# Set-up of quaternions, rows and rotation at other places, second batch's quotients on ScalarE, coefficients copied by GpSimd

## The chip, the cores and the metric

The kernel runs on 1 core of one Trainium2 chip. The metric is the device time of one execution in microseconds. The five engines of a core are named as in the profile: PE is TensorE (matmuls; PEld its weight loads), DVE is VectorE, ACT is ScalarE, POOL is GpSimd, and SP is SyncE, which here issues DMAs. Each engine works through its own instructions in order and waits on the others by semaphores.

## What is computed

Four layers are added to x (8 batches of 256 rows by 256 channels, fp32), one after another. The reference, cut to what matters:

```
def _tc_rmsnorm(x, t, gw, gb, bw, bb):
    g = (t @ gw.T + gb)[:, None, :]; b = (t @ bw.T + bb)[:, None, :]
    return g * x * rsqrt(mean(x * x, -1) + EPS) + b

# layer 0
x = x + _attention(_tc_rmsnorm(x, t, g1w, ...), Wq, Wk, Wv, Wo)        # 16 heads of 16
x0 = x + _swiglu(_tc_rmsnorm(x, t, g2w, ...), gate_w, hid_w, out_w)    # hidden 1024
# layer 1: masked attention, its output normed, scaled and shifted by cond
mod = silu(conditioning) @ Wc.T + bc
x1 = xn * (1.0 + sc[:, None, :]) + shift[:, None, :]
# layer 2: rotation by quaternions, every channel of 4 x 64
q_right_n = _normalize(q_right); q_left_n = _normalize(q_left)
x_rotated = hamilton(q_left_n, hamilton(x_filtered, conj(q_right_n)))
# layer 3: top 2 of 8 experts by a router, each a 3-layer MLP of width 512
return einsum('bseh,bse->bsh', out_e, cw)
```

Layer 2 is one 4 by 4 matrix for each of the 64 quaternion channels; `cond_256` serves as q_left. The kernel builds that matrix once, while the first batches run.

## The kernel before

A batch of 256 rows is worked on as two tiles of 128 partitions. Layer 0's and layer 1's attentions of all batches are cut into blocks (one half of the heads and one half of the keys): a block issues 8 score products s_a into PSUM (L988) and one exponential on ScalarE (L990); the values o_a follow a block later (L1001), and four VectorE instructions turn, divide and turn back the result (tu, inv, on, oT, L1010 to L1018). A function `run` issues a list of blocks. After each block it takes pieces of other work (projections, swiglu products) from a generator until a budget of microseconds is used up; `beside` holds generators of which one step is issued after a given block; `soon` is how many pieces are issued ahead of the function that closes an attention (`after_first`, L1094, or `after_second`, L1164: the outward projection py and what depends on it).

Up to the end of the second step (six blocks: the last two of the second batch, four of the third), the order in which PE, VectorE, ScalarE and GpSimd get their instructions is the order of the program's text; after that only that of PE, VectorE and ScalarE. So a step that is moved in the text is moved in each engine's queue.

The pieces the diff touches:

- `first_norm(b)`, L1045: a batch's first norm in three parts: the squares of two tiles (L878), an rsqrt of 11 small VectorE instructions (L619 to L624: rq_v, rq_y, then three rounds of three), and the quotients xs (L900 on ScalarE, L902 on VectorE or GpSimd).
- `first(b)`: transposes xs, scales it to xT (L924), then projects k (copy kT on ScalarE, L942), q (two products by a scalar on VectorE, qz, L946) and v (copy va on ScalarE, L957). Scores need qz and kT.
- `prepare_quaternions`: squares and sums both quaternions, an rsqrt, four products (19 VectorE instructions), then 32 copies of one column each on GpSimd into lm and rm (L784, L786).
- `set_up_rotation`, a generator of four parts: the matrix rot and the router's share of it on VectorE (L791 to L820), the DMAs that write its coefficients to memory and read them back for all partitions (L822, L824); then the copy to coef (L829) and the products pmc for layer 1's modulation, moved to SBUF as mc (L834); then hall (L851); then shg.
- `set_up_rows`: five iotas on GpSimd and two casts on VectorE for the tables of expert tiles, which are made from round 6 on.
- `second_step`, a generator whose steps are issued beside the six blocks of the second step; between the rotation's parts it takes the fourth batch's norm (`first_turned(3)`), whose row of rstd goes to memory and back by two DMAs (L1063, L1065) and is multiplied in at L1071 (xr).

The banks of PSUM that projections, pmc, pg, ph and phall go to are three, used in turn; a product waits until the bank three before it has been read.

```
        g0 = first(0)
        next(g0)
        keep_busy(2)
        scales()
        do(first_norm(1))
        for _ in g0:
            pass
```

Of the kernel before, what the change touches and what calls it, by code (L numbers as in the profile page):

```python
# [493 lines left out]
def block_kernel(ctx: ExitStack, tc: tile.TileContext, a: dict, out: bass.AP):  # L494
    nc = tc.nc
# [308 lines left out]
    def set_up_rotation():  # L804
        prepare_rotation()

        nc.vector.tensor_tensor(
            wg4s, part["wg4"].rearrange("p (j e) -> p j e", e=E),
            part["rms4"].unsqueeze(2).to_broadcast([P, 4, E]), ALU.mult,
        )  # L810
        for h in range(2):
            r = slice(h * C, (h + 1) * C)
            nc.vector.tensor_copy(rmine[r], rotg[r].rearrange("p j (k h) -> p k h j", h=2)[:, :, h, :])
        turned = work.tile([P, KC, 4, E], F32, tag="raw", bufs=2, name="turned")
        nc.vector.tensor_tensor(
            turned, rmine.unsqueeze(3).to_broadcast([P, KC, 4, E]),
            wg4s.unsqueeze(1).to_broadcast([P, KC, 4, E]), ALU.mult,
        )
        nc.vector.tensor_reduce(gall, turned.rearrange("p k j e -> p k e j"), AX.X, ALU.add)
        nc.vector.tensor_copy(wv1[:, :, D:], gall)  # L820

        nc.sync.dma_start(out=coef_row, in_=rotg[0:C].rearrange("c j i -> c (j i)"))  # L822
        rows_in = wt("x4", [P, C, 4, 4], "coef_in", 1)
        nc.sync.dma_start(  # L824
            out=rows_in.rearrange("p c j i -> p (c j i)"),
            in_=coef_row.rearrange("c w -> (c w)").partition_broadcast(P),
        )
        yield
        nc.scalar.copy(coef, rows_in.rearrange("p c j i -> p i j c"))  # L829

        pm = bank("pmc", (P, 2 * KC, B))
        for k in range(2 * KC):
            nc.tensor.matmul(pm[:, k, :], wcT[:, k * P : (k + 1) * P], silu_c, start=True, stop=True)
        nc.vector.tensor_tensor(mc, pm, part["bcc"].unsqueeze(2).to_broadcast([P, 2 * KC, B]), ALU.add)  # L834
        nc.vector.scalar_tensor_tensor(
            mc[:, KC:], mc[:, KC:], 1.0, part["rsc"].unsqueeze(2).to_broadcast([P, KC, B]), ALU.add, ALU.mult
        )
        scaled = wt("mod", [P, KC, B, E], "scaled")
        nc.vector.tensor_tensor(
            scaled, mc[:, KC:].unsqueeze(3).to_broadcast([P, KC, B, E]),  # L840
            gall.unsqueeze(2).to_broadcast([P, KC, B, E]), ALU.mult,
        )
        yield
        ph = bank("phall", (P, KC, B * E))
        for c in range(KC):
            for k in range(KC):
                nc.tensor.matmul(
                    ph[:, c, :], wo1n[:, k, c * P : (c + 1) * P], scaled[:, k].rearrange("p b e -> p (b e)"),
                    start=k == 0, stop=k == KC - 1,
                )  # L850
        nc.vector.tensor_copy(hall.rearrange("p k b e -> p k (b e)"), ph)  # L851
        ps = bank("pshift", (B, E))
        for k in range(KC):
            nc.tensor.matmul(ps, mc[:, k, :], gall[:, k, :], start=k == 0, stop=k == KC - 1)
        each = work.tile([B, B, E], F32, tag="r_each", bufs=1, name="each")
        nc.vector.tensor_tensor(
            each, ps.unsqueeze(1).to_broadcast([B, B, E]),
            ident[0:B, 0:B].unsqueeze(2).to_broadcast([B, B, E]), ALU.mult,
        )
        yield  # L860
        pb = bank("pshg", (P, B * E))
        nc.tensor.matmul(pb, ones[0:B, :], each.rearrange("p b e -> p (b e)"), start=True, stop=True)
        nc.vector.tensor_copy(shg.rearrange("p b e -> p (b e)"), pb)
        yield
# [172 lines left out]
    def do(parts):  # L1037
        for _ in parts:
            pass
# [5 lines left out]
    def first_norm(b):  # L1045
        s = state[b]
        s["x"] = xs_in.pop(b)
        yield from normed(
            lambda xs: s.update(xs1=xs), s["x"], f"n1_{b}", (nc.scalar, nc.scalar) if b == 0 else (nc.vector, nc.scalar) if b == 1 else nc.gpsimd,
            (nc.scalar, nc.scalar if b else nc.vector),  # L1050
        )

# [287 lines left out]
    def set_up_rows():  # L1340
        full = row("fulli", [NJ, len(BOUNDS)], I32)
        for i, bound in enumerate(BOUNDS):
            nc.gpsimd.iota(full[:, :, i], [[SL, NJ]], base=bound, channel_multiplier=0)
        rows["full"] = row("full", [NJ, len(BOUNDS)])
        nc.vector.tensor_copy(rows["full"], full)
        rows["tno"] = iota_row("tno", NBIG, 1)
# [403 lines left out]
    def chain(*gens):  # L1750
        for g in gens:
            yield from g
# [33 lines left out]
    def once(f, *args):  # L1786
        f(*args)
        yield

    def at_once(*gens):  # L1790
        for g in gens:
            for _ in g:
                pass
        yield
# [10 lines left out]
    with tc.manual_schedule(engines=by_text):  # L1805
        unread = ps_o.tile([P, P], F32, tag="o", name="unread")
        keep_busy(9)
        n1 = first_norm(0)
        next(n1)
        next(n1)  # L1810
        set_up_factors(0)
        set_up_factors(2)
        do(n1)
        keep_busy(3)
        g0 = first(0)
        next(g0)
        keep_busy(2)
        scales()
        do(first_norm(1))
        for _ in g0:  # L1820
            pass
        blank = set_up_slots()
        prepare_condition()
        cond_g = prepare_router()
        finish_slots(*blank)
        def third(b):

            operand = first(b)
            yield next(operand)
            yield from set_up_router(cond_g)  # L1830
            yield from operand

        def take(n, pieces):
            for _ in range(n):
                yield next(pieces)


        operands = first(1)
        run("b", chain(take(1, operands), set_up_condition(), set_up_router(cond_g)), 9.0, rest=False)
        run("b", take(1, operands), 9.0, {0: [at_once(first_norm(2))]}, rest=False)  # L1840
        run("b", iter(()), 0.0)
        run("b", operands, 9.0, rest=False)
        operands = first(2)
        then = run("b", iter(()), 0.0, hold=True)
        run("b", take(1, operands), 9.0, owed=then, soon=1, rest=False)

        def second_step():
            set_up_rows()
            prepare_quaternions()
            yield  # L1850
            rotation = set_up_rotation()
            next(rotation)
            yield
            n1 = first_turned(3)
            next(n1)
            next(n1)
            next(rotation)
            yield
            do(n1)
            next(rotation)  # L1860
            set_up_ones()
            yield
            yield from rotation

        set_up = second_step()
        gaps = [1.9, 4.0, 7.2, 7.2, 7.2, 7.2]
        run("bbbbbb", chain(operands, others(0)), gaps, {n: [set_up] for n in range(5)})
    by_text = {mybir.EngineType.DVE, mybir.EngineType.Activation}
    text_order = ctx.enter_context(ExitStack())
    text_order.enter_context(tc.manual_schedule(engines=by_text))  # L1870
# [1 line left out]
    for i in range(2, B - 1):  # L1872

        placed = {
            2: lambda: once(compare_queries), 4: lambda: at_once(place_choices(0)),
            6: lambda: at_once(place_choices(1)),
        }.get(i, lambda: iter(()))()
        last, rotated = rotated, rotate(i - 2)
        n1 = first_turned(i + 2) if i + 2 < B else iter(())
        n2, r1 = in_parts(i, "n2"), in_parts(i - 2, "r1")  # L1880
        gaps = [7.6, 5.7, 3.8, 5.7, 8.2, 3.8, 2.5, 3.8] if i + 2 < B else [7.6, 3.8, 1.9, 5.7, 7.6, 1.2, 1.9, 3.8]
        starts = {0: [last, n1], 1: [last, n2], 2: [n2]}
        beside = {
            0: [last, n1], 1: [last, n2], 2: [n1], 3: [last], 4: [placed], 5: [r1], 6: [rotated],
            7: [rotated, rotated],
        }
        if i == B - 2:

            early = table("early", (NG - 2) * NTG, EARLY, ALU.is_ge)
            for t in (4, 7):  # L1890
                beside[t].append(early)
        run("bbbbbbbb", others(i - 1), gaps, beside, late_=() if i + 2 < B else (4,), starts=starts)


    pieces = others(B - 2)
# [7 lines left out]
        pl, "s", EARLY, near_end=(next(others_[0]) for _ in range(1)),  # L1903
    )
    n2 = in_parts(B - 1, "n2")
    run("bbbvn", pieces, 3.8, {0: [n2], 2: [early], 3: [early]}, soon=3, rest=False, starts={0: [n2], 1: [n2]})

    next(pieces)
    next(pieces)
# [192 lines left out]
```

## Time and profile before

| what | us |
|---|---|
| median of 5 runs | 711.0 |
| lowest and highest | 707.83, 713.07 |
| the profiled execution, device time | 711.29 |
| its span in the profile | 709.5 |
| VectorE, ScalarE, GpSimd busy | 367.2, 257.2, 178.4 |

The granted TensorE clock over the span is 0.994 of full speed. Times in rows of the profile are microseconds from the span's start; a row gives start, length, engine, line, operation, output and inputs with shapes, and how often it stands there in a row. The part that the diff touches first lies between 9 and 77 us (first two steps), the last one at 384 to 398 us (end of the seventh batch's swiglu).

### The profile page before, as it was taken

What the parts mean: (1) busy time and instruction counts of PE and PEld (TensorE: products, weight loads), DVE (VectorE), ACT (ScalarE), POOL (GpSimd) and SP (SyncE); (2) the same over time, 40 slices, a digit from 0 to 9 for tenths busy, and PEclk for the clock granted to TensorE, in tenths of its full rate; (3) what the DMA queues carried; (4) which work ended last, traced back from release to release, by engine and by line L of the source; (5) the groups of instructions that cost most, each with busy time, mean ns of one, the idle gap of its engine ahead of it and who ended that gap; (6) DMA issues with size and microseconds to landing.
All of it is one profiled execution on the core that took longest, in us unless ns stands there. A gap on an engine that the chain in (4) does not pass through costs nothing.

```text
span 709.5 us, 11183 instructions
## 1 busy us (share of the span) xinstructions
PE 690.1 (97%) x4258; PEld 531.0 (75%) x4258; DVE 367.2 (52%) x1166; ACT 257.2 (36%) x411; POOL 178.4 (25%) x222
## 2 busy tenths in 40 slices
PE   9979999999999999999999999999999999999994
PEld 7546876766766766766676786688888998999894
DVE  5474346476478486377575686688321222222221
ACT  4655135345354354355434335322111212222220
POOL 5330501001000141100230016224373332342213
PEclk9999999999999999999999999999999999999998
DMA  9414001002021000020000151737585866576712
GB/s 298 151 33 80 1 1 38 1 16 38 1 75 38 1 18 7 1 75 1 2 16 1 25 193 25 290 130 213 144 274 158 239 232 204 168 259 199 249 25 29
DMA packets 28879, 70.02 MB, mean 99 GB/s; under 512 B 9032, under 2 KB 22224, under 8 KB 26384
## 3 DMA queue, kind: packets, MB, share of 16 engines
q1 hardware_dynamic: 20032, 57.70, 25.0%
q0 software_dynamic: 8496, 11.32, 7.2%
q8 instruction: 35, 0.57, 0.3%
q14 instruction: 28, 0.23, 0.1%
q10 hardware_dynamic: 288, 0.18, 0.1%
HBM read 59.67 MB, written 9.53 MB: 98 GB/s over the span
## 4 chain that ended last, share of the span: by engine, by line
PE 83%; DVE 7%; DMA 2%; issue 1%; ACT 1%; POOL 1%; POOLq 0%; DVEq 0%; ACTq 0%
PE ph_a_rest L1526 10%; PE pd L1141 8%; PE ph_a_p L1526 7%; PE s_a L988 7%; PE pg L1128 6%; PE o_a L1001 6%; PE ph L1128 6%; PE ph_s_sure L1526 5%; PE pe_a_rest L1556 3%; PE pk_a L932 3%; PE pq_a L932 3%; PE pe_a_p L1556 3%; PE pv_a L962 2%; PE pe_s_sure L1556 2%; PE py L1024 2%; PE py L1174 2%
## 5 line engine op out<-in xcount | busy, mean ns | idle before, releaser
L990 ACT ACTIVATE pe_a<-s_a 128x2048 f32<-128x2048 f32 x64 | 120.1, 1876 | 96.0 <-PE s_a L988 95.9
L988 PE MATMUL s_a<-qz_a,kT_a 32*128 32x512 f32 x512 | 73.2, 639 | 2.3 <-DVE qz_a L946 1.0
L1128 PE MATMUL pg<-xT_n,gate_wT 128*128 128x256 f32 x256 | 62.1, 385 | 1.2 <-DVE xT_n L924 0.6
L1128 PE MATMUL ph<-xT_n,hid_wT 128*128 128x256 f32 x256 | 61.8, 384 | 0.3 <-DVE sg L1134 0.3
L1001 PE MATMUL o_a<-pe_a,va 128*32 128x256 f32 x1024 | 61.9, 382 | 0.0
L1001 PEld LDWEIGHTS o_a<-pe_a,va 128*32 128x32 f32 x1024 | 30.0, 110 | 39.9 <-issue 23.4
L1141 PE MATMUL pd<-out_wT,hT 128*128 128x256 f32 x256 | 59.1, 384 | 0.4 <-DVE hT L1136 0.4
L1128 PEld LDWEIGHTS ph<-xT_n,hid_wT 128*128 128x128 f32 x256 | 47.6, 190 | 14.7 <-issue 2.7
L1128 PEld LDWEIGHTS pg<-xT_n,gate_wT 128*128 128x128 f32 x256 | 47.3, 190 | 13.8 <-issue 3.2
L1141 PEld LDWEIGHTS pd<-out_wT,hT 128*128 128x128 f32 x256 | 47.7, 190 | 13.1 <-issue 3.2
L1010 DVE STREAM_TRANSPOSE tu_a<-o_a 128x512 f32<-128x512 f32 x32 | 22.8, 712 | 51.9 <-PE o_a L1001 51.9
L1526 PE MATMUL ph_a_rest<-h_a_rest,w_a_rest 128*128 128x256 f32 x224 | 49.6, 380 | 0.0
L1526 PEld LDWEIGHTS ph_a_rest<-h_a_rest,w_a_rest 128*128 128x128 f32 x224 | 42.0, 190 | 5.4
L1101 POOL TENSOR_TENSOR xy<-y,x 128x512 f32<-128x512 f32 x8 | 10.2, 1270 | 139.7 <-DVE rq_v_n L619 57.5
L1537 DVE TENSOR_SCALAR h_a_rest<-ph_a_rest,w_a_rest 128x256 f32<-128x256 f32 x28 | 13.6, 484 | 57.3 <-PE ph_a_rest L1526 56.3
L1314 POOL DMA_INDIRECT slots<-rec,posi x32 | 32.0, 1001 | 23.4 <-issue 7.3
L988 PEld LDWEIGHTS s_a<-qz_a,kT_a 32*128 32x128 f32 x512 | 20.3, 183 | 21.3 <-issue 12.7
L1526 PE MATMUL ph_a_p<-h_a_p,w_a_p 128*128 128x192 f32 (+2 forms) x224 | 36.0, 319 | 0.0
L1132 ACT ACTIVATE th<-pg 128x512 f32<-128x512 f32 x32 | 19.0, 594 | 44.9 <-PE pg L1128 44.8
L1535 ACT ACTIVATE h_a_rest<-ph_a_rest,w_a_rest 128x256 f32<-128x256 f32 x28 | 13.3, 473 | 60.7 <-DVE h_a_rest L1537 60.7
L1526 PEld LDWEIGHTS ph_a_p<-h_a_p,w_a_p 128*128 128x128 f32 x224 | 34.9, 191 | 0.1
L1134 DVE SCALAR_TENSOR_TENSOR sg<-th,pg 128x512 f32<-128x512 f32 x32 | 21.9, 684 | 22.8 <-ACT th L1132 22.8
(352 smaller groups left out, 1181.7 us busy)
## 6 DMA issues: line engine op xcount, KB each, us to landing
w_a_rest<-in_experts SPq DMA_DIRECT2D x7, 2180.0 KB, 8.9
w_a_p<-in_experts SPq DMA_DIRECT2D x7, 2180.0 KB, 9.2
w_s_sure<-in_experts SPq DMA_DIRECT2D x4, 2180.0 KB, 9.7
w_s_early<-in_experts SPq DMA_DIRECT2D x1, 2180.0 KB, 8.3
mod<-mod_rows SPq DMA_DIRECT2D x8, 256.0 KB, 3.3
tokens<-x SPq DMA_DIRECT2D x4, 512.0 KB, 3.5
out<-x SPq DMA_DIRECT2D x4, 512.0 KB, 4.4
x<-in_x SPq DMA_DIRECT2D x7, 256.0 KB, 2.7
```

The source lines that it names most:

```text
L932: nc.tensor.matmul(pp[:, c, :], w[:, k, c * P : (c + 1) * P], xT[:, k, :], start=k == 0, stop=k == KC - 1)
L988: nc.tensor.matmul(sc[:, j], kT[r, c, kc * P : (kc + 1) * P], qz[r, c], start=True, stop=True)
L990: nc.scalar.activation(pe, sc, AF.Exp)
L1001: nc.tensor.matmul(o[32 * i : 32 * i + 32, qd, :], va[:, kc, 8 * c + 4 * qd + i].rearrange("p a d -> p (a d)"), pe[:, 2 * qd + i // 2, i % ...
L1010: nc.vector.transpose(turned.rearrange("p q j a d -> p (q j a d)"), o.rearrange("p q s -> p (q s)"))
L1128: nc.tensor.matmul(ps[:, j, :], w[:, k, o : o + P], yT[:, k, :], start=k == 0, stop=k == KC - 1)
L1132: nc.scalar.activation(th, pg, AF.Tanh, scale=0.5)
L1134: nc.vector.scalar_tensor_tensor(sg, th, 1.0, pg, ALU.add, ALU.mult)
L1141: nc.tensor.matmul(pd[:, t, :], hT[:, c, t * P : (t + 1) * P], out_w[:, c, :], start=c == 0, stop=c == HID // P - 1)
L1314: sc = nc.gpsimd.indirect_dma_start(out=slots, out_offset=bass.IndirectOffsetOnAxis(ap=posi[:, t : t + 1], axis=0), in_=rec[:, t, :], in_o ...
L1526: nc.tensor.matmul(ph[:, c - c0, 0:many], w[:, o : o + P], src[:, k, 0:many], start=k == 0, stop=k == n_in - 1,)
L1556: nc.tensor.matmul(pos[q][0:p, q, :], h2[:, k, q * p : (q + 1) * p], w[:, o : o + D], start=k == 0, stop=k == MC - 1,)
```

## The change

- The second batch's norm is taken apart: squares and rsqrt are issued ahead of the first batch's k, its quotients after the first batch's q and ahead of its v. Both its quotients are made by ScalarE; VectorE made one of them before.
- `prepare_quaternions` is issued beside the second block, where the third batch's norm stood; that norm moves beside the third block.
- `set_up_rows` leaves the second step and is issued beside the fifth block of round 3.
- `second_step` has a step less and starts beside the second of its six blocks: its other steps stay beside the same blocks.
- The copy to coef is made by GpSimd.
- In the run that ends the seventh batch's swiglu, `soon` is 2 for 3.

```
@@ set_up_rotation
         yield
-        nc.scalar.copy(coef, rows_in.rearrange("p c j i -> p i j c"))
+        nc.gpsimd.tensor_copy(coef, rows_in.rearrange("p c j i -> p i j c"))
@@ first_norm
-            lambda xs: s.update(xs1=xs), s["x"], f"n1_{b}", (nc.scalar, nc.scalar) if b == 0 else (nc.vector, nc.scalar) if b == 1 else nc.gpsimd,
+            lambda xs: s.update(xs1=xs), s["x"], f"n1_{b}", nc.gpsimd if b > 1 else nc.scalar,
             (nc.scalar, nc.scalar if b else nc.vector),
@@ block_kernel, start
         scales()
-        do(first_norm(1))
-        for _ in g0:
-            pass
+        n1 = first_norm(1)
+        next(n1)
+        next(n1)
+        next(g0)
+        next(g0)
+        do(n1)
+        do(g0)
         blank = set_up_slots()
@@ first step
         run("b", chain(take(1, operands), set_up_condition(), set_up_router(cond_g)), 9.0, rest=False)
-        run("b", take(1, operands), 9.0, {0: [at_once(first_norm(2))]}, rest=False)
-        run("b", iter(()), 0.0)
+        run("b", take(1, operands), 9.0, {0: [once(prepare_quaternions)]}, rest=False)
+        run("b", iter(()), 0.0, {0: [at_once(first_norm(2))]})
         run("b", operands, 9.0, rest=False)
@@ second step
         def second_step():
-            set_up_rows()
-            prepare_quaternions()
-            yield
             rotation = set_up_rotation()
             next(rotation)
             yield
...
         gaps = [1.9, 4.0, 7.2, 7.2, 7.2, 7.2]
-        run("bbbbbb", chain(operands, others(0)), gaps, {n: [set_up] for n in range(5)})
+        run("bbbbbb", chain(operands, others(0)), gaps, {n: [set_up] for n in range(1, 5)})
@@ rounds 2 to 6
         placed = {
-            2: lambda: once(compare_queries), 4: lambda: at_once(place_choices(0)),
+            2: lambda: once(compare_queries), 3: lambda: once(set_up_rows), 4: lambda: at_once(place_choices(0)),
             6: lambda: at_once(place_choices(1)),
@@ after round 6
-    run("bbbvn", pieces, 3.8, {0: [n2], 2: [early], 3: [early]}, soon=3, rest=False, starts={0: [n2], 1: [n2]})
+    run("bbbvn", pieces, 3.8, {0: [n2], 2: [early], 3: [early]}, soon=2, rest=False, starts={0: [n2], 1: [n2]})
```

## The prediction

> **What bounds the kernel now.** I read the busy times first, then TensorE's waits one by one, then the rows of time around each wait the diff touches.
>
> ```profile
> PE 690.1 (97%) x4258; PEld 531.0 (75%) x4258; DVE 367.2 (52%) x1166; ACT 257.2 (36%) x411; POOL 178.4 (25%) x222
> ```
>
> TensorE (PE) works for 690.1 of 709.5 us. Nothing in the diff removes a large matmul, so all it can win or lose is TensorE's idle time, and the clock TensorE gets after idling. The table of who TensorE waited for, cut to the first 60 us, shows four waits the diff can reach (in all, times, longest):
>
> ```profile
> PE py L1024 <- DVE oT_a L1018: 2.8, 1, 2.8
> ...
> PE s_a L988 <- DVE qz_a L946: 1.0, 1, 1.0
> PE s_a L988 <- ACT pe_a L990: 0.3, 1, 0.3
> PE s_a L988 <- DVE half_c L695: 0.2, 1, 0.2
> ```
>
> The largest in the rows of time (start, length, engine, what; in brackets the idle time before it and who ended it):
>
> ```profile
> 48.13 0.17 DVE L791 TENSOR_TENSOR rot<-lm,rm 128x16 f32<-128x16 f32 x1 [1.47 <-POOL lm L784]
> ...
> 51.20 0.17 DVE L820 COPY wv<-gall 128x16 f32<-128x16 f32 x1
> 51.28 0.71 DVE L1010 STREAM_TRANSPOSE tu_a<-o_a 128x512 f32<-128x512 f32 x1
> ...
> 53.27 2.92 PE L1024 MATMUL py<-L_WoT_turned,oT_a 128*128 128x256 f32 x6 [2.83 <-DVE oT_a L1018]
> ...
> 56.24 0.69 DVE L1100 TENSOR_TENSOR y<-py,x 128x512 f32<-128x512 f32 x1 [3.02 <-PE py L1024]
> ```
>
> VectorE (DVE) waits for GpSimd's 32 tiny copies of lm and rm, then works off the rotation, and only then transposes attention's output, for which TensorE stands still. The table by stretches (length, five engines' busy time, then TensorE's granted clock) shows that the stall has a second price:
>
> ```profile
> 46.80:50.00 3.20, 3.19 (x41) 1.52 (x42) 1.44 (x8) 1.99 (x2) 2.17 (x19) 1.00 0.02 5
> ...
> 53.20:54.20 1.00, 0.93 (x2) 0.83 (x3) 0.02 (x1) 0.00 (x0) 0.00 (x0) 0.50 0.87 360
> ...
> 55.20:56.20 1.00, 1.00 (x4) 0.35 (x2) 0.00 (x0) 0.00 (x0) 0.00 (x0) 0.50 0.00 0
> ...
> 520.00:522.00 2.00, 0.73 (x5) 0.36 (x3) 0.48 (x1) 0.47 (x1) 1.62 (x1) 1.00 1.04 442
> ```
>
> After 2.83 us idle the clock is 0.50 for some 3 us; after stalls of 1.00 us (46.8) and 1.27 us (521) it stays 1.00.
>
> **The change, part by part.** The sum is a position against the old one at each landmark.
>
> Start. The second batch's squares, rsqrt and quotients are issued around the first batch's k and q. VectorE loses its half of the quotients, 0.35 us, which stood ahead of qz: qz starts right after the rsqrt, 13.04 for 13.30, and ends 14.44. TensorE is free at 12.74 + 1.89 = 14.63 and started its scores at 14.86: -0.23. ScalarE's two quotients (0.91, as the first batch's at 6.98) end by 13.94; they are transposed at 15.93, and the va copy behind them starts at 14.72, so they cost nothing with 0.8 us to spare. The kT copy gets ahead of them: free.
>
> Quaternions, now after the second scores. 19 VectorE instructions, 41.77 to 45.35 = 3.58 us, go into the 3.82 us that VectorE is idle before 22.65. The 32 GpSimd copies, 44.88 to 48.97 = 4.1 us, run from 22.2 to 26.3, behind the table's DMA issues (ending 21.41) and ahead of the third batch's quotients. Those start at 28.2 for 25.07, take 1.88, and are needed at 33.37: hidden.
>
> Third batch's norm, now one step later. Its two squares on ScalarE (1.05 us) no longer delay the exponential at 22.52; that starts 1.2 after its scores (20.89), at 22.09, and the scores waiting for it move from 24.43 to 24.00. But its 11 rsqrt instructions now stand behind attention's four on VectorE. These start at 23.96 and take 1.94 (24.70 to 26.64 before), so rsqrt runs from 25.9 and pushes qz 2.05 us on (22.65 to 24.70), to 27.95:
>
> ```profile
> 27.54 1.41 DVE L946 TENSOR_SCALAR qz_a<-pq_a,par 128x512 f32<-128x512 f32 x2 [0.90 <-PE pq_a L932]
> ...
> 29.16 1.14 PE L988 MATMUL s_a<-qz_a,kT_a 32*128 32x512 f32 x8
> ```
>
> qz ends 29.36, scores follow 0.14 later (46.67 to 46.81), at 29.50, while TensorE is ready at 28.73: a new stall of 0.77. Net here +0.34.
>
> Second step without quaternions and rows ahead of qz. TensorE comes at 45.80 + 0.34 = 46.14; qz starts at 41.99 + 1.93 = 43.92, ends 45.33, no wait: -0.67 for the old 46.81. The rotation's first part, 48.13 to 51.37 = 3.24, starts at 45.33 with lm and rm long there, and ends 48.57, before attention's output (47.21 + 2.0 = 49.21). oT is ready 1.95 later, py goes on at 51.20: -2.07. A stall of 51.20 - 49.78 = 1.42 us remains, since nothing is placed between the two. Nearest rows 1.27 (clock kept) and 2.83 (clock lost): kept. Then y comes 1.61 after py resumes, as at 34.22 to 35.83, not 2.97: 52.81, **-3.43**. If the clock falls after all, -2.07.
>
> Coefficients on GpSimd. ScalarE loses this row:
>
> ```profile
> 59.06 1.92 ACT L829 COPY coef<-coef_in 128x1024 f32<-128x1024 f32 x1
> ```
>
> That brings the next exponential forward and removes the 0.33 us wait at 64.80, but TensorE then waits at 71.17 for hall, behind xr, whose row of rstd went through two DMAs issued after VectorE's rsqrt: nothing won. GpSimd gains the copy, right behind xy. The trace doesn't show such a copy. By element, a memset of 1024 takes 0.95 us, the xT quotients with two scalars 0.55 per 256, va's 1.56 per 512, the xs quotients 0.94 per 256: 0.95 to 3.75 us for 1024. I take 2.2, the row of 0.55, one read and one write. It would be free if GpSimd's time were all, but:
>
> ```profile
> 108.70 0.16 DVE L619 TENSOR_SCALAR rq_v_n<-ss_n 128x2 f32<-128x2 f32 x1
> 108.87 1.27 POOL L1101 TENSOR_TENSOR xy<-y,x 128x512 f32<-128x512 f32 x1 [20.06 <-DVE rq_v_n L619]
> 108.90 1.26 DVE L620 TENSOR_SCALAR rq_y_n<-rq_v_n 128x2 int32<-128x2 int32 x1
> ...
> 110.19 0.16 DVE L622 SCALAR_TENSOR_TENSOR rq_p_n<-rq_y_n,rq_v_n 128x2 f32<-128x2 f32 x1
> ```
>
> rq_y, 0.17 us alone, is held until GpSimd's xy ends; the same at 162.07, 215.23 and 269.46. The copy starts as xy ends, 2.05 us after y starts (58.29 - 56.24); rq_v ends there too, rq_y would follow 0.04 later. So rq_y is held for the copy, and ends D - 0.2 = 2.0 late (D the copy's length). Queued behind it on VectorE: the rest of this rsqrt, the fourth batch's rsqrt, mc. For mc's bank TensorE waits at 62.48; for rstd's DMAs, xr and hall at 71.17. **+2.0**, between 0 (the copy misses rq_y) and 3.55.
>
> Clock, once more. TensorE, ready for that matmul some 0.6 us ahead of an unheld mc, now stalls 2.6 us, near the 2.83 that lost the clock. At 0.50, py's six took 2.92 for 1.30: 1.6 lost. From 62.48 to 71.17 TensorE has 0.23 + 0.33 of waiting that absorbs part: +1.0 if it falls, 0 if not. I take 0.5.
>
> [...]
>
> Rows set up later. Two VectorE casts (0.28 us) and five iotas (0.5 us on GpSimd) move from the second step to round 3, where TensorE shows no wait between 120 and 231 us; hidden, 0.28 at most.
>
> End of round 7, soon=2. The outward projection py1 goes ahead of the last quarter of pd. Before: pd, py1, transposes, then 0.60 idle at 397.44 for xT_n, behind two copies and four table instructions. After, those are done earlier and xT_n waits only for x2, 0.7 us after pd: first product at some 397.1. -0.3, between -0.35 and +0.3.
>
> Sum: -3.43 + 2.0 + 0.5 - 0.3 = -1.23. The profiled execution took 711.29 us (span 709.5 and 1.8 around it), 0.3 over the median: 710.1, or **709.8** against the median of 711.0.
>
> **Rivals.** *The copy holds nothing.* It starts too late or early for rq_y, or such a copy doesn't hold VectorE. -3.43 - 0.3 = -3.73: 707.3. For it: the race is decided by 0.04 us. Against: GpSimd won it in each of the four rows named.
>
> *The copy holds VectorE for long.* ScalarE's copy of this stepped pattern took 1.92 for 1024, about what its exponentials take for 2048 (1.88): the step doubles it. If GpSimd's slower rows (3.1 and 3.75) double as well, D is 6.2 to 7.5. Then +6.0 to +7.3 in place of 2.0 and 1.0 of clock: 714.3 to 715.6. It ends slower than before from D = 2.9 with the clock lost, 3.9 with it kept. Against: no GpSimd row is that slow.
>
> *The wait only moves.* qz at 27.95 slips further or the 1.42 us stall loses the clock too: -2.07 + 2.0 + 0.5 - 0.3, 711.1.
>
> **How the numbers follow.** What a measurement of this kernel can tell is about 0.5%, 3.55 us: below 707.45 or above 714.55. Forecast 0.46 (within); copy harmless 0.26, of which 0.22 lies below; copy long 0.20, 0.18 above; wait only moved 0.08, within. Faster 0.22, same 0.60, slower 0.18. The forecast's own range, D from 0.95 to 3.75 and both clocks, is 708.0 to 712.4. The whole range goes from 706.4 (copy harmless, and the new 0.77 us stall absent too: -3.43 - 0.77 - 0.35) to 714.3, the near end of the long copies.
>
> **What would show it.** Right: 2.8 gone from TensorE's waits for oT, some 1.4 left with a clock of 1.00; a new wait for qz near 29 of about 0.8; rq_y of about 2 us beside the coefficients' copy; a wait for mc of 2 to 3 us. Wrong: rq_y at 0.17 there, a copy far from 2.2 us, or a clock of 0.50 after py.

## Result, and the profile after

The changed kernel takes 708.83 us (median of 44 runs, 707.02 to 713.75), the kernel before 711.15 us on the same chips (86 runs). The ratio of the runs is 0.9986, 95% interval 0.9975 to 0.9996: 1.0 us less, between 0.3 and 1.8, which is inside the 0.5% that counts as no change. It is the ratio of the means (709.76 and 710.78 us); the times of both kernels lie in two groups some 3 us apart, and the two medians lie in different ones, so they differ by 2.3. The forecast was 709.8 us, and no change.

The profiled execution took 711.83 us (span 710.0), longer than the median and than the 711.29 us of the profile before. So spans are not compared here. I compare three landmarks inside a profile, all starts on TensorE: the first scores (`s_a`), py going on after its stall, and the first scores of the second layer.

| | first scores | py goes on | second layer | first to second layer | py to second layer |
|---|---|---|---|---|---|
| before | 14.86 | 53.27 | 97.95 | 83.09 | 44.68 |
| changed | 18.26 | 54.69 | 100.25 | 81.99 | 45.56 |

Between the first scores and the second layer the change gains 1.10 us. It gains 1.98 up to py (38.41 to 36.43) and gives back 0.88 after it. The changed kernel's first scores come 3.4 us later, ahead of anything the diff could have done there; that is taken up with the fourth experiment.

TensorE's waits in the changed kernel (who waited for whom: in all, times, longest):

```profile
PE pg L1128 <- DVE mc L834: 2.2, 1, 2.2
...
PE py L1024 <- DVE oT_a L1018: 1.4, 1, 1.4
PE ph L1128 <- DVE sg L1134: 0.7, 1, 0.7
PE s_a L988 <- DVE qz_a L946: 0.6, 1, 0.6
```

py's 2.8 became 1.4, the old 1.00 us wait for qz became 0.6 at another place, and the wait for mc, 0.40 before, became 2.2. Two rows of the kernel before, for the third:

```profile
58.34 0.17 DVE L620 TENSOR_SCALAR rq_y_n<-rq_v_n 128x2 int32<-128x2 int32 x1
...
62.48 1.99 PE L1128 MATMUL pg<-xT_n,gate_wT 128*128 128x256 f32 x8 [0.40 <-DVE mc L834]
```

The changed kernel's rows of time for the three, and for what lies behind the third:

```profile
33.05 1.14 PE L988 MATMUL s_a<-qz_a,kT_a 32*128 32x512 f32 x8 [0.58 <-DVE qz_a L946]
...
54.69 1.56 PE L1024 MATMUL py<-L_WoT_turned,oT_a 128*128 128x256 f32 x6 [1.43 <-DVE oT_a L1018]
...
57.06 1.27 POOL L1101 TENSOR_TENSOR xy<-y,x 128x512 f32<-128x512 f32 x1 [15.29 <-DVE y L1100]
58.16 0.19 DVE L619 TENSOR_SCALAR rq_v_n<-ss_n 128x2 f32<-128x2 f32 x1 [1.18 <-ACT junk_n L878]
...
58.27 1.94 POOL L829 COPY coef<-coef_in 128x1024 f32<-128x1024 f32 x1
58.46 1.78 DVE L620 TENSOR_SCALAR rq_y_n<-rq_v_n 128x2 int32<-128x2 int32 x1
```

GpSimd's copy starts right behind xy, takes 1.94 us, and VectorE's rq_y of two elements a row lasts 1.78 beside it, for 0.17 in the kernel before. Everything behind rq_y on VectorE, down to mc, is late by that. The stretches around the wait for mc (length, busy time of TensorE, of its weight loads, VectorE, ScalarE and GpSimd, then the granted clock, the share of the DMA engines and GB/s):

```profile
62.00:64.00 2.00, 0.00 (x0) 0.00 (x0) 1.65 (x13) 1.39 (x3) 0.00 (x0) 1.00 0.00 0
64.00:66.00 2.00, 1.79 (x6) 1.48 (x7) 1.83 (x6) 0.00 (x0) 0.00 (x0) 0.72 0.52 35
66.00:68.00 2.00, 2.00 (x9) 1.73 (x7) 0.08 (x1) 0.60 (x1) 0.00 (x0) 0.50 1.05 53
68.00:70.00 2.00, 2.00 (x21) 1.14 (x24) 0.69 (x1) 0.00 (x0) 0.00 (x0) 0.92 0.64 75
```

TensorE idles through a whole stretch, and then its clock is at 0.50 for some 3.4 us: (1 - 0.72) x 2 / 0.5 = 1.1 us of the second stretch, all of the third, 0.3 of the fourth. In this part the kernel before lost its clock once too, after py's stall of 2.83 us (0.50 from 53.10 to 56.51 us); between these two profiles the loss moved from py to pg.

### The profile page after: what moved, and what is told of

It is laid out like the page before. It is cut to its first block, busy times and chain, and to the rows that moved or that the text cites. A ratio compares the mean times of both kernels' runs of the same rounds, so it can differ in the third digit from the quotient of the medians.

```text
span 710.0 us, 11186 instructions
## 1 busy us (share of the span) xinstructions
PE 693.1 (98%) x4258; PEld 534.8 (75%) x4258; DVE 369.1 (52%) x1165; ACT 256.1 (36%) x411; POOL 180.5 (25%) x223
## 4 chain that ended last, share of the span: by engine, by line
PE 89%; DVE 8%; ACT 1%; issue 1%; POOL 0%; POOLq 0%; DVEq 0%; ACTq 0%
PE ph_a_rest L1526 10%; PE s_a L988 8%; PE pd L1141 8%; PE ph_a_p L1526 7%; PE o_a L1001 7%; PE pg L1128 7%; PE ph L1128 6%; PE ph_s_sure L1526 6%; PE pk_a L932 4%; PE pq_a L932 3%; PE pe_a_rest L1556 3%; PE pe_a_p L1556 3%; PE pe_s_sure L1556 2%; PE py L1024 2%; PE pv_a L962 2%; PE pv_a L954 2%
```

## The experiments

Twelve runs were made, on four occasions. On three of them the kernel before itself took 733 to 738 us, with added stalls of TensorE and lost clock in the profiles from some 250 us on (in e1, 4.82 us idle of the 40 from 340 to 380 us, at a clock of 0.91; in the kernel before's profile 0.92 of the 149 from 231 to 380, at 1.00), whose cause is not shown; so times are given only as ratios to the kernel before on the same chip, and the landmarks used lie before 110 us, but for those of the last round, which lie between two of these stalls.

| | first scores | first to second layer | py to second layer | ratio to before (95%) |
|---|---|---|---|---|
| e1 copy back on ScalarE | 15.51 | 79.27 | 42.82 | 0.9969 (0.9943 to 0.9994) |
| e2 before, copy on GpSimd | 15.08 | 84.32 | 45.90 | 1.0019 (0.9995 to 1.0044) |
| e3 soon=3 | 18.64 | 83.50 | 47.05 | 1.0001 (0.9970 to 1.0032) |
| e4 start as before | 18.35 | 81.99 | 45.55 | 0.9993 (0.9965 to 1.0021) |
| e5 copy later on GpSimd | 18.18 | 80.00 | 43.57 | 0.9964 (0.9942 to 0.9986) |
| e6 stall filled, 18 | 15.08 | 81.84 | 45.40 | 0.9995 (0.9969 to 1.0020) |
| e7 copy in four | 14.97 | 80.48 | 44.06 | 0.9989 (0.9957 to 1.0021) |
| e8 better version | 14.73 | 77.15 | 41.38 | 0.9914 (0.9887 to 0.9941) |
| e9 stall filled, 9 | 15.05 | 81.06 | 44.63 | 0.9962 (0.9944 to 0.9981) |
| e10 changed kernel again | 15.20 | 80.75 | 44.32 | 0.9969 (0.9948 to 0.9990) |
| e11 before, moves alone | 18.23 | 79.27 | 42.83 | 0.9940 (0.9918 to 0.9963) |
| e12 better version again | 14.87 | 77.82 | 42.04 | 0.9927 (0.9901 to 0.9953) |

### The copy taken off GpSimd

```diff
-        nc.gpsimd.tensor_copy(coef, rows_in.rearrange("p c j i -> p i j c"))
+        nc.scalar.copy(coef, rows_in.rearrange("p c j i -> p i j c"))
```

> The changed kernel with the coefficients' copy back on ScalarE; everything else of the change stays. Theory (GpSimd's copy holds VectorE's rq_y, so mc comes late, TensorE stalls 2.24 us for its bank and loses its clock): rq_y back to 0.17 us, the wait for mc 0.3 to 0.8 us, the clock 1.00 from 62 to 72, and from the batch's first scores to the first scores of the second layer (83.1 before, 82.0 changed) 79.5 to 80.7 us; the time about 2 us under the changed kernel's 708.8, some 706.8. Rival (the wait only moves: something else is as late there, the rows of rstd through the DMAs or ScalarE's own copy ahead of its exponential): 81.5 to 82.5 us between those scores, a wait of 1.5 us or more for another tile in place of mc, and 708 to 709 us.

Rows of its profile:

```profile
55.73 0.17 DVE L620 TENSOR_SCALAR rq_y_n<-rq_v_n 128x2 int32<-128x2 int32 x1
...
56.38 1.92 ACT L829 COPY coef<-coef_in 128x1024 f32<-128x1024 f32 x1
...
59.86 1.99 PE L1128 MATMUL pg<-xT_n,gate_wT 128*128 128x256 f32 x8 [0.63 <-DVE mc L834]
```

rq_y is back to 0.17, the wait for mc is 0.63, and the clock is 1.00 from 44 to 76 us. 79.27 us is a little under the theory's range: the copy on GpSimd cost that profile of the changed kernel 2.7 us (81.99 - 79.27), and the rival's 81.5 to 82.5 us falls. The time does not decide: 0.9969 is what the rival expected (708 to 709 us are 0.996 to 0.997), and the theory's 706.8 us, 0.994, lies just below its interval. It is the rows and the landmarks that speak for the theory. The second rsqrt on VectorE (rq_v) starts 5.62 us after py here (57.58 - 51.96) and 7.23 in the changed kernel (61.92 - 54.69): 1.61 us of plain delay. The rest of the 2.7, 1.1 us, I put down to the clock, which was at 0.50 for 3.4 us in the changed kernel's profile.

### The copy alone

The same line changed in the kernel before, the other way round.

> The kernel before with one edit: the coefficients' copy on GpSimd. Theory (the copy holds VectorE): rq_y beside the copy 1.7 to 2.0 us in place of 0.17, the wait for mc from 0.40 to about 2.1 us, 83.1 us between the first scores of the two layers to 84.8 (clock kept) or 86 (clock lost), and a time 1.7 to 2.9 us over the kernel before. Rival (the copy misses rq_y when py comes late as in the kernel before, or such a copy holds nothing): rq_y 0.17, 82.7 to 83.1 us, and the time within 0.4 us of the kernel before.

```profile
58.44 1.91 POOL L829 COPY coef<-coef_in 128x1024 f32<-128x1024 f32 x1
...
58.56 1.82 DVE L620 TENSOR_SCALAR rq_y_n<-rq_v_n 128x2 int32<-128x2 int32 x1
```

VectorE is held as the theory says (1.82), and 84.32 us is 1.23 more than before, above the rival's range and below the theory's 84.8. But no wait for mc shows, since TensorE itself was slow: py's stall of 2.83 us, the same as in the kernel before, cost the clock for three times as long.

```profile
52.00:54.00 2.00, 0.50 (x1) 0.50 (x2) 1.34 (x4) 0.00 (x0) 0.00 (x0) 0.69 0.40 125
54.00:56.00 2.00, 2.00 (x6) 1.35 (x4) 0.00 (x0) 0.00 (x0) 0.00 (x0) 0.50 0.40 137
56.00:58.00 2.00, 2.00 (x9) 1.65 (x8) 0.69 (x1) 0.72 (x3) 0.76 (x1) 0.50 0.00 0
58.00:60.00 2.00, 2.00 (x10) 0.65 (x9) 1.64 (x2) 1.31 (x6) 2.00 (x2) 0.50 0.20 35
60.00:62.00 2.00, 2.00 (x8) 1.51 (x5) 1.69 (x10) 1.69 (x1) 0.35 (x1) 0.50 0.29 100
62.00:64.00 2.00, 2.00 (x8) 1.67 (x7) 1.68 (x11) 1.50 (x4) 0.00 (x0) 0.75 0.00 0
```

By the same reckoning, 1.24 + 8 + 1.00 = 10.24 us at 0.50. The delay of mc lay beside that. So this run shows the hold, and not cleanly its price; its time, 1.0019 (0.9995 to 1.0044), settles no sign.

### The last round

```diff
-    run("bbbvn", pieces, 3.8, {0: [n2], 2: [early], 3: [early]}, soon=2, rest=False, starts={0: [n2], 1: [n2]})
+    run("bbbvn", pieces, 3.8, {0: [n2], 2: [early], 3: [early]}, soon=3, rest=False, starts={0: [n2], 1: [n2]})
```

> The changed kernel with soon=3 again in the last round. Theory (what soon=2 wins at the first product of the second half, 0.2 us, is given back at the wait for sg behind GpSimd's xs): from the scores at 384 to those at 443 (58.41 us before, 58.58 changed) 58.4 us, the wait for xT_n of 0.6 back, that for sg 0.67 to about 0.3, time within 0.4 us of the changed kernel. Rival (soon=2 is worth what was predicted, 0.3 us, or the DMA wait of 1.27 us at 522 went because of it): 58.9 us, or the DMA wait back and 1.3 us more.

The 58 us announced reach into a stall that the occasion added, so I take shorter distances. From the scores just ahead of pd's first part (382.15 us before, 384.44 changed) to the next batch's first scores it takes 22.47 us in each of four profiles with soon=3 (before, e2, e3, e11) and 22.29 or 22.30 in changed, e1, e4 and e10 with soon=2: soon=2 wins 0.18. To the scores 22 us further, 45.07, 45.22, 45.44 and 45.07 us in the first four, 45.24, 45.25, 45.07 and 45.24 in the others: the gain is gone there on the mean (45.20 for 45.20). What eats it is the wait for sg (0.32 to 0.68 us), but not as I expected: in this run it was 0.68 with soon=3. It does not belong to soon=2, and what sets it I have not settled. The early part of this profile, not edited, shows the clock lost for two stretches:

```profile
64.00:66.00 2.00, 1.40 (x6) 1.21 (x7) 1.76 (x8) 0.00 (x0) 0.00 (x0) 0.91 0.06 8
66.00:68.00 2.00, 2.00 (x9) 1.73 (x7) 0.47 (x1) 0.57 (x1) 0.00 (x0) 0.50 1.18 61
68.00:70.00 2.00, 2.00 (x13) 1.47 (x16) 0.69 (x1) 0.02 (x1) 0.00 (x0) 0.50 0.61 98
70.00:72.00 2.00, 2.00 (x19) 0.41 (x15) 0.71 (x2) 0.73 (x1) 0.00 (x0) 0.50 0.64 161
72.00:74.00 2.00, 2.00 (x30) 1.04 (x23) 0.51 (x3) 1.14 (x1) 1.85 (x3) 0.88 0.00 0
```

That is 0.36 + 6 + 0.48 = 6.84 us, after a stall of 2.25 us, and 47.05 us from py to the second layer for the changed kernel's 45.56.

### The start

```diff
-        n1 = first_norm(1)
-        next(n1)
-        next(n1)
-        next(g0)
-        next(g0)
-        do(n1)
-        do(g0)
+        do(first_norm(1))
+        for _ in g0:
+            pass
```

with the second batch's quotients on VectorE and ScalarE again.

> The changed kernel with the second batch's norm as before: all of it ahead of the first batch's k and q, half of the quotients on VectorE. Theory (this part is worth a few tenths; the 3.4 us by which the first scores stood later in the changed kernel's profile come from matmuls of the first 14 us that took up to twice as long in that execution, and not from the change): first scores either near 14.9 or near 18.3, by chance, two groups of run times some 3 us apart as in both kernels, and a median within 0.6 us of the changed kernel's. Rival (the new order delays the start by 3.4 us): first scores near 14.9 and the time about 3 us under the changed kernel's, some 705.5.

The first scores came at 18.35 with the old order. Over all 14 profiles they come at 14.73 to 15.51 (nine) or at 18.18 to 18.64 (five), and both orders are in both groups: e4 and e11 have the old start and are late. The rival falls. What is late is TensorE itself. First the kernel before, then the changed one:

```profile
5.51 1.95 PE L636 MATMUL paff<-small_in,aff_w 64*128 64x8 f32 x16
...
7.39 0.94 PE L1802 MATMUL unread<-ident 128*128 128x128 f32 x6
```

```profile
5.64 3.58 PE L636 MATMUL paff<-small_in,aff_w 64*128 64x8 f32 x16
...
9.15 1.65 PE L1802 MATMUL unread<-ident 128*128 128x128 f32 x6
```

The same 16 products take 3.58 us for 1.95; they take 3.58 in all five late profiles and 1.95 to 2.28 in the others. The view gives a granted clock of 1.00 there in both, but that is not a record: the trace of the kernel before has its first record of the clock, of 1.00, at 5.31 us, that of the changed kernel at 13.69, and the view counts what lies ahead of it as 1.00. The products of k (pk_a) show what the clock was. First the kernel before, then the changed one:

```profile
9.18 2.00 PE L932 MATMUL pk_a<-xT_n,L_WkT 128*128 128x256 f32 x8
```

```profile
12.29 2.58 PE L932 MATMUL pk_a<-xT_n,L_WkT 128*128 128x256 f32 x8
```

In the changed kernel's profile these products start 0.427 us apart up to 13.57 us and 0.216 from 13.85 on: TensorE had half its speed up to the record at 13.69. The first products of all (`unread`) start 0.213 us apart in both profiles; in the kernel before's, products of that kind start 0.111 apart from 7.61 on, behind its record at 5.31. In the other late profiles (e3, e4, e5, e11) the eight products of pk_a, from 12.29 or 12.30 on, take 2.50 to 2.96 us, in the nine early ones 1.99 or 2.00. So in a late start TensorE is slow for longer, by 8.38 us between these two profiles (13.69 - 5.31), with either order of the text.

### The copy somewhere else on GpSimd, and in pieces

```diff
             do(n1)
+            late_copy.pop()()
             next(rotation)
```

where late_copy holds the unchanged copy, taken out of the step before.

> The changed kernel with the copy still on GpSimd, but issued one step later, behind the fourth batch's quotients on GpSimd. Theory (it is the meeting of the copy and rq_y that costs, not GpSimd's doing the work): rq_y 0.17 us, the wait for mc 0.3 to 0.8 us, the clock 1.00, and from the resumption of py to the first scores of the second layer (44.7 us before, 45.6 changed, 42.8 with the copy on ScalarE) 42.3 to 43.0 us, unless the copy meets another instruction of VectorE that TensorE waits for. Rival (any place on GpSimd holds VectorE as much, since it always has a small instruction to hold): 45 us or more, with a held instruction of 1 us or more and a TensorE wait behind it.

```profile
71.54 1.92 POOL L831 COPY coef<-coef_in 128x1024 f32<-128x1024 f32 x1
71.60 2.15 DVE L1016 TENSOR_TENSOR on_a<-tu_a,invs 128x256 f32<-128x256 f32 x1
...
74.86 1.99 PE L1130 MATMUL pg<-xT_n,gate_wT 128*128 128x256 f32 x8 [0.55 <-DVE hT L1138]
```

rq_y took 0.17, the wait for mc 0.63, the clock stayed. The copy now held another instruction, on_a, for 2.15 us (0.42 alone). Of the 1.73 us lost there, TensorE waited 0.55 for hT behind it. So 43.57 us, above the theory's 43.0 and below the rival's 45: it is the meeting that counts, but there is a meeting at this place too, with some slack behind it.

```diff
-        nc.gpsimd.tensor_copy(coef, rows_in.rearrange("p c j i -> p i j c"))
+        for i in range(4):
+            nc.gpsimd.tensor_copy(coef[:, i], rows_in[:, :, :, i].rearrange("p c j -> p j c"))
```

> The changed kernel with GpSimd's copy cut into four of 256 elements, some 0.5 us each. Theory A (VectorE gets its turn between two instructions of GpSimd): rq_y is held for 0.3 to 0.6 us, the wait for mc falls to about 1.0 us, and py to second layer takes 43.3 to 44.2 us. Theory B (a waiting GpSimd instruction goes ahead of a waiting VectorE one each time, as the copy did behind xy): rq_y is held for all four, 1.7 to 2.2 us, the wait for mc 2.2 us or more, and 45.3 us or more.

GpSimd's four pieces and VectorE's instructions of the same time:

```profile
54.98 2.28 POOL L830 COPY coef<-coef_in 128x256 f32<-128x256 f32 x4
...
55.16 0.46 DVE L620 TENSOR_SCALAR rq_y_n<-rq_v_n 128x2 int32<-128x2 int32 x1
...
55.66 0.51 DVE L622 SCALAR_TENSOR_TENSOR rq_p_n<-rq_y_n,rq_v_n 128x2 f32<-128x2 f32 x1
56.20 0.52 DVE L623 TENSOR_TENSOR rq_p_n<-rq_p_n,rq_y_n 128x2 f32<-128x2 f32 x1
56.76 0.52 DVE L624 SCALAR_TENSOR_TENSOR rq_y_n<-rq_p_n,rq_y_n 128x2 f32<-128x2 f32 x1
57.31 0.16 DVE L622 SCALAR_TENSOR_TENSOR rq_p_n<-rq_y_n,rq_v_n 128x2 f32<-128x2 f32 x1
```

rq_y lasts 0.46 us, as theory A has it, but the next three last 0.51 or 0.52 each, for the 0.16 that such an instruction takes once the four pieces are through (57.26): by these lengths, each of the four waited for one piece of 0.57 (2.28 / 4). So the wait for mc was 1.99 us, not 1.0; the second rsqrt started 6.98 us after py (58.37 - 51.39), a delay of 1.36 for the 1.61 of the whole copy. A's range for the time held (44.06), but mostly because the clock stayed at 1.00.

### What the lost clock costs

```diff
+                if i == 3:
+                    idle = ps_s.tile([P, 4, 2, S], F32, tag="s", name="idle")
+                    for _ in range(18):
+                        nc.tensor.matmul(idle[:, 0, 0, 0:P], ident, ident, start=True, stop=True)
```

in a generator around the pieces of the step, behind the first pg and ph. These products are added to the computation; nothing reads them.

> The changed kernel with 18 products of the identity with itself, whose result nobody reads, where TensorE waits for mc (some 2 us of work): the delay stays, the idle time goes. Theory (of the copy's price of 2.7 us, some 1.6 is the later mc and 1.1 the clock lost after the stall): mc's wait 0 to 0.5 us, the granted clock 1.00 from 60 to 72, and 43.9 to 44.6 us from py to the second layer's scores (45.6 changed). Rival (the clock costs nothing, since other waits bound the next 6 us): 45.3 to 45.9 us with the clock at 1.00.

A mis-sized experiment: the 18 products took 4.18 us and ended 1.6 us after mc was there (62.65 against 61.02). The clock stayed at 1.00, and 45.40 us lies in the rival's range, but that 1.6 is in it; without it I estimate 43.8. Half as many:

> As the filled stall, with 9 products of the identity in place of 18, since the 18 took 4.2 us and ran 1.6 us past mc. Theory (some 1.6 us of the copy's price is the later mc, 1.1 the clock): the 9 take some 2.1 us and end about where mc does, the clock stays 1.00, and from py to the second layer's first scores 43.7 to 44.3 us (45.6 changed, 42.8 with the copy on ScalarE). Rival (the clock's fall costs nothing): 45.3 us or more.

2.17 us of products, a wait for mc of 0.23 left, the clock at 1.00, and 44.63 us, over the theory's 44.3: a wait for hall of 0.47 us came in behind the DMAs of rstd. That alone doesn't price the clock, and the next run, of the changed kernel with no edit, shows why.

> The changed kernel itself, beside the others on one chip. Theory: wait for mc 2.24 us, the clock lost after it for one or two of the stretches of 3.4 us seen so far, 45.5 us from py to the second layer's scores with one, 47.1 with two; the time 0.997 to 1.000 of the kernel before. Rival (the clock is lost only now and then after 2.2 us): a clock of 1.00 there and about 44 us.

```profile
61.14 1.99 PE L1128 MATMUL pg<-xT_n,gate_wT 128*128 128x256 f32 x8 [2.24 <-DVE mc L834]
```

The same stall of 2.24 us, and the clock stayed at 1.00. My expectation gave it one or two lost stretches; the rival was right. So the same instructions after the same stall have 44.32 us from py to the second layer with the clock kept (e10), 45.56 and 45.55 with one stretch lost (changed, e4), 47.05 with two (e3). One stretch costs 1.24 us, two cost 2.73. And the copy without the clock costs 44.32 - 42.83 = 1.49 (42.83 is e11's, with the copy on ScalarE).

Why e10 kept the clock is not shown. In the traces of the kernel before and of the changed kernel the first three records of the granted clock, of 1.00, 0.50 and 1.00, last 47.79, 3.41 and 648.53 us and 51.20, 3.41 and 638.29: 14, 1 and 190, and 15, 1 and 187 times 3.413. In the changed kernel the clock fell at 64.89, 0.69 us after the end of the stall (61.96 to 64.20), and by the stretches at 65.64 in e3, 1.04 after it, and at 65.08 in e4, 0.78 after it. In e10 it was 1.00 in every stretch from 50 to 76 us, around a stall of 58.90 to 61.14. That the place of the stall between such multiples decides is a guess of mine; no run moved it on purpose.

### The moves alone

The kernel before, with the quaternions in the first step, the third batch's norm one step later and the rows in round 3; its start, its ScalarE copy and its last round kept.

```diff
-        run("b", take(1, operands), 9.0, {0: [at_once(first_norm(2))]}, rest=False)
-        run("b", iter(()), 0.0)
+        run("b", take(1, operands), 9.0, {0: [once(prepare_quaternions)]}, rest=False)
+        run("b", iter(()), 0.0, {0: [at_once(first_norm(2))]})
...
-            set_up_rows()
-            prepare_quaternions()
-            yield
```

> The kernel before with the moves alone: quaternions to the first step, the third batch's norm one step later, rows to round 3; the coefficients on ScalarE, the start and the last round as before. Theory (these moves are all that the change wins): py's stall 1.4 us with the clock at 1.00, the wait for qz 0.6 us, 79.0 to 79.7 us from the first scores to those of the second layer (83.1 before, 79.3 with all of the change but the copy), and a time 3 to 4 us under the kernel before. Rival (the start's edit carries a part of it): 80 us or more.

79.27 us, the same as with all of the change but the copy (e1), and a ratio of 0.9940 (0.9918 to 0.9963): the moves are the gain, 3.8 us, and the copy takes a good part of it away. The start's edit and soon=2 add nothing to this distance; what the edit does ahead of the first scores does not count in it. How the gain divides among the three moves was not run.

### A better version

From the changed kernel: the copy on ScalarE behind hall's products; mc's products and mc ahead of py; hall ahead of xr on VectorE; the third batch's rsqrt behind qz.

```diff
-        nc.gpsimd.tensor_copy(coef, rows_in.rearrange("p c j i -> p i j c"))
+        late_copy.append(lambda: nc.scalar.copy(coef, rows_in.rearrange("p c j i -> p i j c")))
...
+        third_norm = first_norm(2)
+        run("b", iter(()), 0.0, {0: [third_norm]})
+        def with_norm(pieces):
+            yield next(pieces)
+            do(third_norm)
+            yield from pieces
+        run("b", with_norm(operands), 9.0, rest=False)
...
             next(n1)
             next(n1)
+            yield
             next(rotation)
-            yield
             do(n1)
-            next(rotation)
+            late_copy.pop()()
...
+        run("bbbbbb", chain(operands, others(0)), gaps, {n: [set_up] for n in range(1, 5)}, starts={2: [rotation]})
```

> A version made from what the runs showed: the coefficients' copy on ScalarE, in its idle time behind the next two tanh; the products for mc and mc itself ahead of py, in TensorE's 1.4 us stall for oT; hall's copy ahead of xr on VectorE; the third batch's rsqrt and quotients behind qz. Theory: the wait for qz at 30 to 33 us (0.58) and that for mc (0.63) gone, py's stall down from 1.43 to about 0.4, the clock 1.00; from the first scores to the second layer's first scores 76.6 to 77.6 us (83.1 before, 82.0 changed, 79.3 with the copy on ScalarE alone); a time 5 to 6 us under the kernel before. Rival (the waits only move: pt_n waits for the third batch's quotients, pg waits for hall behind xr's DMAs): 78.5 to 79.5 us, no faster than with the copy on ScalarE alone.

```profile
28.85 1.14 PE L989 MATMUL s_a<-qz_a,kT_a 32*128 32x512 f32 x8
...
48.37 1.05 PE L834 MATMUL pmc<-silu_c,WcT 64*128 64x8 f32 x8
...
50.50 1.56 PE L1025 MATMUL py<-L_WoT_turned,oT_a 128*128 128x256 f32 x6 [0.45 <-DVE oT_a L1019]
...
58.89 1.10 PE L848 MATMUL phall<-scaled,wo1n 128*128 128x64 f32 x8 [0.38 <-DVE sg L1135]
```

No wait for qz, no wait for mc, 0.45 us left of py's stall, since 1.05 us of mc's products now lie in it. 77.15 us, inside the theory's range, and 0.9914 (0.9887 to 0.9941) of the time before.

> The better version a second time, on another occasion. Theory: 77.0 to 77.3 us from the first scores to the second layer's, the clock 1.00 from 44 to 76 us, and 0.989 to 0.994 of the kernel before. Rival (the first result owed part of its size to its runs): 0.995 or more at the same distance between the scores.

0.9927 (0.9901 to 0.9953) the second time, as expected. The distance missed the narrow range, 77.82: TensorE waited 0.73 us for hT, because xr, and VectorE's work behind it, started 0.68 later after the first scores (66.04 - 14.87 against 65.22 - 14.73), when the row of rstd had come through its DMA.

## Why the prediction was right, point by point

- **Start, -0.23.** Not seen. Among profiles with the early start the old order has its first scores at 14.86 and 15.08, the new one at 14.73 to 15.51. qz still stands behind the second batch's rsqrt, and that waits for x's transfer: the first squares began at 9.78 us in the kernel before and at 10.82 in e1, where the first scores waited 1.28 us for VectorE. I took the transfer's moment from one execution as fixed.
- **Quaternions, hidden.** Right: the GpSimd copies ended at 29.7, the third batch's quotients ran from 31.86 and were needed at 37.24.
- **Third norm, a new wait of 0.77.** 0.58. From the first scores to those after the wait 14.79 us, predicted 14.87 (29.50 - 14.63).
- **py.** A stall of 1.43 (predicted 1.42), and py goes on 36.43 us after the first scores (36.57). The clock stayed at 1.00 after it in every profile with this stall (ten, of 1.43 or 1.44). This step carried the forecast, and it held to 0.14 us.
- **The coefficients' copy, +2.0.** The mechanism was right to the instruction; the size was 1.49 (e10 against e11). The copy took 1.94 for the 2.2 assumed, rq_y 1.78 for 2.0, the wait for mc 2.24 for 2.6.
- **The clock, +0.5.** A mean that no execution shows: 0, 1.24 or 2.73. The bounds of 0 to 1.0 were too narrow at the top, and the prediction went by the stall's length (2.6 us, near 2.83), where stalls of 2.24 and 2.25 us went with all three.
- **Rows later.** Hidden: TensorE was busy for 105.96 of the 106 us from 125 to 231 in both kernels.
- **The last round, -0.3.** -0.18 at the next scores, nothing on the mean 22 us later.
- **A wait not in the sum.** The kernel before's profile has a DMA wait of 1.27 us at 521.95 that is in none of the changed kernel's, e9's, e10's and e11's. Waits of 1.0 to 1.5 us for the same kind of transfer stand in e2, e8 and e12, so they go with neither kernel; I took the before profile as if it were typical there.
- **The range.** The forecast's own upper end, 712.4, is 711.8 by the two terms that it names, D of 3.75 and the lost clock; the last round's +0.3 makes the rest.

Without the copy the moves gave -3.82 between the landmarks, for a predicted -3.20 (-3.43 counted from the start, less its -0.23). 1.96 of that is there when py goes on, 1.37 comes with y, which no longer waits for a slow py (1.60 us after py for 2.97), and 0.49 after it, of which the sum had nothing. With the terms as measured, -3.82 + 1.49 with the clock kept, and 1.24 more with one stretch of it lost, the change is worth -2.3 to -1.1 us (with two, as in e3, +0.4); the runs say -1.0, and -2.2 on the occasion of e10. Copy, clock and moves were off by half a microsecond each and in part against each other, which is luck that a range of 8 us doesn't show.

**The rivals.** The copy that holds nothing falls with the changed kernel's rq_y of 1.78, the long copy with its 1.94; whether the stepped pattern is what made ScalarE's copy slow no run shows, since none copied coef without it. The wait that only moves is right about 0.58 us of it and no more.

## What to carry to other kernels

Price a step moved to another engine by the instruction it will run beside, not by that engine's idle time: GpSimd was idle for 15 us ahead of xy, and its copy of 1.94 us still cost 1.49, since an instruction of 0.17 us on VectorE had a chain behind it for which TensorE stood still. A stall has a price of its own length and a second one, 0 to 2.73 us here for the same 2.24, that the text of the kernel does not fix, so fill it with work that has to be done anyway (mc's products in py's stall) before shortening anything else. And when two executions of one kernel differ by more than the change is worth, compare distances between landmarks, not spans.

## What the runs showed of the hardware

**The clock was at 0.50 in lengths of some 3.4 us.** The stretches at 0.50 add up to 3.40 us (before), 3.44 (changed), 6.84 (e3) and 10.24 (e2): one, one, two and three of some 3.4 us. Between 50 and 76 us, the clock fell after 2.83 us of idle time both times (before, e2), after 2.24 to 2.25 in three of four profiles (changed, e3, e4, but not e10), after 1.99 (e7) and after 1.43 or 1.44 (ten profiles) never. In the 3.41 us ahead of each of the five falls TensorE was idle for 2.65 us (before), 2.24 (changed, e4), 2.25 (e3) and 2.1 (e2). What made it three lengths in e2, and none in e10, was not tried.

**GpSimd's copies held instructions of VectorE.** rq_y, with one input and two elements a row, lasted 1.78 us beside the copy of 1.94 (changed) and 0.17 without it (e1). In e7 rq_y and the three instructions behind it lasted 0.46 to 0.52 us, for 0.16 or 0.17, beside four pieces of 0.57. In e5 an instruction of VectorE with two inputs was held too, on_a for 2.15 us, for 0.42, beside the copy of 1.92. What holds them, and which others would be held, these runs do not show.

**The start has two speeds.** In five of 14 profiles the 16 products of paff took 3.58 us, in the others 1.95 to 2.28, and the first scores came at 18.18 to 18.64 us, in the others at 14.73 to 15.51, with either order of the start. In the changed kernel's profile TensorE was busy for 12.19 of the 13.69 us before its speed rose, in the kernel before's for 3.81 of 5.31; why the one rose so much later was not tried. The three profiles that lost the clock after the stall of 2.24 or 2.25 us started late (18.26, 18.64, 18.35), e10 early (15.20). Between the changed kernel's two profiles, of 710.0 and 705.9 us, the start is 3.06 us (18.26 against 15.20), and the lost clock 1.24: together the whole of their difference, to 0.2 us. The start alone is more than the change is worth.
